# Latent attention on one core: DMA transposes in block 0, an fp16 output stage and moved pieces

## The chip, the cores and the metric

The kernel runs on one NeuronCore of one Trainium2 chip. The metric is the device time of one execution in microseconds; a kernel's time is the median of its runs.

## The reference

For 2048 tokens of 512 channels the program computes one transformer layer: latent attention (16 heads, head width 128 plus 64 rotary columns, causal), a residual and a layer norm, then a linear layer with a residual and a second layer norm.

```python
cq = rms_norm(x @ w_qa.T, q_a_ln_w)                  # 2048 x 384
q_nope, q_pe = split((cq @ w_qb.T) by head)          # 128 + 64 columns per head
ckv = x @ w_kva.T                                    # 2048 x (128 + 64)
ckv_l, k_pe = rms_norm(ckv[:, :128], kv_a_ln_w), rotate(ckv[:, 128:])
k_nope, v = split((ckv_l @ w_kvb.T) by head)         # 128 + 128 columns per head
scores = (q_full @ k_full.T) * 192 ** -0.5           # causal
attn = softmax(scores) @ v @ w_o.T                   # 2048 x 512
y = layernorm(x + attn)
out = layernorm(y + y @ (weight * scale_weight[:, None]).T + bias)
```

The inputs and the output are fp32. The kernel writes most operands as a sum of a high and a low part and adds three products (high by high, high by low, low by high).

## The kernel before

**Tiling.** The 2048 tokens are four blocks of 512 queries (`b`), the 16 heads eight pairs (`p`), each block four tiles of 128 (`qt` or `t`). A pair's scores against the keys up to the diagonal lie in PSUM, their softmax is written as fp16 high and low parts (`hl`), and SP's DMA queue turns these by `dma_start_transpose` into `PT` (block 0) or `ring` (blocks 1 to 3), from which TensorE multiplies them by the latent values `V`. So the attention leaves, for each pair, a latent output `o` of 128 x 1024 per block, which is stored in DRAM (`ot_d`) and read back in the output stage. `values` runs some units behind the softmax (`lag` is 4 in block 0, at most 3 later).

**Block 0** (0 to about 283 us) also does all projections. A written plan places pieces of them between the units of attention: "F" takes a piece of the query projections, "X" one tile of `project_x`, "W" a piece of the weight preparation. `project_x(hb)` handles 256 tokens: for each of two tiles of 128 it multiplies x into the latent keys (`kvr`), the rotary key (`kp`) and the latent queries (`pc`); the reciprocal norms `rk` are taken; `cq_finish` writes the scaled queries (`nq`, L364), `kv_finish` the scaled keys (`nk`) and, split in two, `V`. TensorE then turns `nq` (three 128 x 128 transposes a tile, `turn_cq`, L377) and `nk` and `kp` (`turn_k`, L384 and L385). ScalarE and VectorE split what was turned into `cqst` and `Kn`; `cqst` is stored to `cq_d`, for the block's queries later. The turns of a tile are run after the products of the next one (`turns`, `last_turn`).

**Blocks 1 to 3** (about 283 to 1284 us) are attention: scores (L626), the exponential (L679 on ScalarE), the split of the probabilities (L700 on ScalarE, L703 on VectorE), values (L756), and between them the next pair's query products (L584) and rotary products (L497, multiplied by the cosines and sines on VectorE, L502). In the last pair of block 3, `prepare_output` starts the output stage: it loads `wo`, the latents of block 0, and multiplies the value weights into `w_o` (`value_output`, L286, products `ps_wo`, result `wvo`). Eight steps `k` make up a pair there; `at` says at which of them a `filler` is taken. A load that is put off (`put_off`) is issued by SP ahead of the next transposes.

**Output stage** (about 1284 us to the end). For each block the eight pairs are added up in four accumulators `acc` (one for each tile `t`, L1057): 6 products of 512 columns a pair and tile, in fp32r, 24 a pair. Each pair's latents are loaded (`latent_load`) and split into `oh` (ScalarE, L74) and `ol` (VectorE, L75) by `latent_split`, one pair ahead. Then `residual` adds x (L1148), `first_norm` takes mean and variance on VectorE (L1138, L1140), their power of -1/2 on GpSimd (L292, L293), and the norm on VectorE (L1143). `ffn` turns the result (`tp`, L1159), splits it (`xt`), adds the bias on GpSimd (`xb`, L1163), multiplies by `fw` (12 products, L1169), adds, norms and stores. The ffn pieces of a block are taken between the products of the next block (`late`, `advance`); TensorE's order there is the program's own. In the last block the tiles are finished one after another, with pairs 2 to 7 split ahead (`ohl` holds those of pairs 4 to 7).

**What orders the work.** Every engine runs its own instructions in order. Where the program does not fix it (`manual_schedule`, `keep_in_program_order`), a scheduler chooses the order of each engine when the kernel is built.

Of the kernel before, what the change touches and what calls it, by code (L numbers as in the profile page):

```python
# [19 lines left out]
P = 128  # L20
# [14 lines left out]
C_TOP = 20100.0  # L35
TINY = 1.0e-30
# [18 lines left out]
def mla_block(ctx: ExitStack, tc: tile.TileContext, a, out):  # L55
# [10 lines left out]
    def split16(src, h, l, scale):  # L66

        nc.scalar.activation(h, src, AF.Copy, scale=scale)
        nc.vector.scalar_tensor_tensor(l, src, scale, h, ALU.mult, ALU.subtract)  # L69
# [11 lines left out]
    cq_d = [dram.tile([P, 2, LT, QB], F16, name=f"cq_d{b}") for b in range(NB)]  # L81
# [21 lines left out]
    kvln_o = const.tile([P, 1], F32, name="kvln_o")  # L103
    nc.vector.tensor_scalar_mul(kvln_o, kvln, 1.0 / (V_UP * P_UP))
# [14 lines left out]
    V = [kv.tile([P, 2, 4, P], F16, name=f"V{b}") for b in range(NB)]  # L119
# [3 lines left out]
    with tc.tile_pool(name="ps_w", bufs=1, space=PSUM) as ps_w:  # L123
        ramp = V[3][:, 0].rearrange("p t d -> p (t d)")
        nc.vector.memset(ramp, 0.0)
        idle = ps_w.tile([P, 512], F32, name="idle")
        for _ in range(10):
            nc.tensor.matmul(idle, ramp[:, :P], ramp, start=True, stop=True)
# [39 lines left out]
    def first_scales():  # L168

        sq = small.tile([P, 1], F32, tag="sq1", name="sq1")  # L170
        nc.vector.tensor_tensor(sq, kvln, kvln, ALU.mult)
        tot = small.tile([P, 1], F32, tag="tot", name="tot")
        column_total(tot, sq, 1)
        root(kvn, tot)
        nc.vector.tensor_scalar(kvn, kvn, C_TOP, None, ALU.mult)

# [104 lines left out]
    def value_output(p, pool, tag):  # L281

        wvo = state["wvo"][p]
        for j in range(2):
            ps = pool.tile([P, HID], F32, tag=tag, name=f"ps_wo{2 * p + j}")
            nc.tensor.matmul(ps, state["wv"][:, 2 * p + j], state["wo"][2 * p + j], start=True, stop=True)  # L286
            split(ps, wvo[:, 0, j, :], wvo[:, 1, j, :], kvln_o)
            yield

# [52 lines left out]
    def kv_finish(hb, i, kvr, rk):  # L342
# [4 lines left out]
        vh, vl = V[b][:, 0, t, :], V[b][:, 1, t, :]  # L347
# [18 lines left out]

    def inverse_rms(ms, n=2):
# [11 lines left out]

    def turn_k(hb, flip, k):  # L380
# [7 lines left out]
        if hb < 2:  # L388
            split16(kf, Kp0[:, 0, cols], Kp0[:, 1, cols], ks[0])
        split16(pt[:, 0].rearrange("p a c -> p (a c)"), Kn[:, 0, cols], Kn[:, 1, cols], K_UP)  # L390
        nc.scalar.activation(Kr[:, cols], kf, AF.Copy)
        if hb >= 2:
            nc.scalar.activation(junk[:, :256], kf, AF.Square, accum_out=ksum[:, hb + 2 : hb + 3])
# [14 lines left out]

    def project_x(hb, wkv, wqa):

        b, half_of = hb // 2, slice(hb % 2 * 256, hb % 2 * 256 + 256)
        x, csk = xsplit.pop(hb)
        flip = []
        st = pa2.tile([P, 2, LT, 256], F16, tag="st", name=f"cqst{hb}")

        def turn(i, nq):
            turn_cq(hb, i, nq, st[:, :, :, i * P : (i + 1) * P], "m")
            if i:
                nc.sync.dma_start(cq_d[b][:, :, :, half_of], st)
                turn_k(hb, flip, "m")  # L420

        for i in range(2):
            ms = small.tile([P, 2], F32, tag="ms", name="ms")
            kvr, kp = kv_products(hb, i, x, wkv, csk, "m", ms[:, 0:1])
            pc = cq_products(hb, i, x, wqa, "m", ms[:, 1:2])
            rk = inverse_rms(ms)
            nq = cq_finish(pc, rk[:, 1:2])
            flip.append((kv_finish(hb, i, kvr, rk[:, 0:1]), kp))
            last_turn()
            turns.append(lambda i=i, nq=nq: turn(i, nq))  # L430
            if i == 0:
                next_x(hb + 1)
# [33 lines left out]
    def load_block(b):  # L466
        if b == NB:
            return
        cq = prj.tile([P, 2, LT, QB], F16, tag="cq", name=f"cq{b}")
# [22 lines left out]
    def rope_products(w, cq, cs, prod, ps, x, cols):  # L492

        n = 0
        for lt in range(LT):
            for i, k in ((0, 0), (0, 1), (1, 0)):
                nc.tensor.matmul(  # L497
                    ps, w[:, i, lt, x * P : (x + 1) * P], cq[:, k, lt, cols], start=n == 0, stop=n == 3 * LT - 1
                )
                n += 1  # L500
        for k in range(2):
            nc.vector.tensor_tensor(prod[:, k, x, cols], ps, cs[:, k ^ x, cols], ALU.mult)  # L502
# [37 lines left out]
    def project_pe(b, g):  # L540
# [7 lines left out]
        for x in range(2):  # L548
            ps = psum["m"].tile([P, QB], F32, tag="m", name=f"ps_pe{b}_{g}_{x}")
            rope_products(w, cq, cs, prod, ps, x, every)  # L550
# [28 lines left out]
    def nope_products(w, cq, qn, ps, j, cols, scale):  # L579

        n = 0
        for lt in range(LT):
            for i, k in ((0, 0), (0, 1), (1, 0)):
                nc.tensor.matmul(  # L584
                    ps, w[:, i, lt, j * P : (j + 1) * P], cq[:, k, lt, cols], start=n == 0, stop=n == 3 * LT - 1
# [159 lines left out]
    def values(b, p, qt, nk, PT):  # L745
# [5 lines left out]
        for k in range(kts):  # L751
# [3 lines left out]
            for i, l in ((0, 0), (0, 1), (1, 0)):  # L755
                nc.tensor.matmul(  # L756
                    ps[:, :256], vt[:, i, k % 4, :], v[:, :, l, k, :], start=n == 0, stop=n == 3 * kts - 1
# [50 lines left out]
    with tc.manual_schedule(engines={ET.PE}):  # L808
# [17 lines left out]
        def turn_queries(hb, nqs, k):  # L826
            for i, nq in enumerate(nqs):
                o = hb * 256 + i * P
                turn_cq(hb, i, nq, state["cq"][:, :, :, o : o + P], k)
# [45 lines left out]
    def rest_of_x():  # L875
        for i in range(2, 8):
            yield from project_x(i, wkv, wqa)
        last_turn()
        yield
# [26 lines left out]
    def units(pool, ring, b):  # L906
        lag = min(ring.shape[1] // (2048 * (b + 1)) - 1, 3) if b else 4

        for p in range(NPAIR):
# [15 lines left out]
            if b == NB - 1 and p == NPAIR - 1:  # L925
# [4 lines left out]
                state["wvo"] = [pcr.tile([P, 2, 2, HID], F32R, name=f"wvo{p}", bufs=1) for p in range(EARLY)]  # L930
                for i in range(EARLY):
                    fillers.append(value_output(i, psum["m"], "m"))
                at = (3, 4, 6, 7)
            for qt in range(4):
# [25 lines left out]
                else:  # L960
                    for j in range(2):
# [8 lines left out]
                        if 2 * qt + j in at:  # L970
                            fill()
                        run_values(lag)
# [34 lines left out]
    EARLY = 2  # L1007
    ohl = []

    def latent_load(b, p, by=nc.sync.dma_start):  # L1010
        o = state["o", b, p] = state["pcr"].tile([P, 4, 256], F32, tag="o", name=f"o{b}_{p}")
        by(o, ot_d[b][p])

    def latent_split(b, p):
        if b == NB - 1 and p >= 4:
            oh, ol = ohl[p - 4]
        else:
            oh = state["pcr"].tile([P, 4, 256], F32R, tag="oh", name=f"oh{b}_{p}")
            ol = state["pcr"].tile([P, 4, 256], F32R, tag="ol", name=f"ol{b}_{p}")
        split(state.pop(("o", b, p)), oh, ol)  # L1020
        return oh, ol

    def latent(b, p):
        latent_load(b, p)
        return latent_split(b, p)
# [8 lines left out]
    def prepare_output(b, p, k):  # L1034
# [6 lines left out]
        if p == NPAIR - 1:  # L1041
            if k == 0:
                load_wo(0, blk, "qn", put_off)
            if k in (0, 1):
                latent_load(0, k, put_off)
            if k == 4:
                load_wo(1, state["pcr"], "wo")
            if k in (2, 5):
                cuts[0, k // 3] = latent_split(0, k // 3)
# [3 lines left out]
    def accumulate(acc, p, t, oh, ol):  # L1053
        for j in range(2):
            c = slice(j * P, (j + 1) * P)
            for n, (l, i) in enumerate(((oh, 0), (oh, 1), (ol, 0))):
                nc.tensor.matmul(  # L1057
                    acc,
                    l[:, t, c],
                    state["wvo"][p][:, i, j, :],  # L1060
# [22 lines left out]
    with tc.manual_schedule(engines={ET.PE, ET.SP}), ExitStack() as ctx_f:  # L1083
        for b in range(1, NB):
            with ExitStack() as ctx_s:
# [7 lines left out]
                units(pools, ring, b)  # L1093
# [5 lines left out]
        wvo += [pcq.tile([P, 2, 2, HID], F32R, name=f"wvo{EARLY + i}") for i in range(2)]  # L1099
# [21 lines left out]
    wvo += [pc.tile([P, 2, 2, HID], F32R, name=f"wvo{p}") for p in range(EARLY + 2, NPAIR - 1)]  # L1121
    wvo.append(state["pcr"].tile([P, 2, 2, HID], F32R, tag="wo", name="wvo7", bufs=1))
# [4 lines left out]
    fw = pc.tile([P, 2, KT, HID], F32R, name="fw")  # L1127
    ohl[:] = [[pc.tile([P, 4, 256], F32R, name=f"ohl{p}_{i}") for i in range(2)] for p in range(4)]

    def load_fw(kt):  # L1130
        raw = pc.tile([P, HID], F32, tag="xb", name=f"fraw{kt}", bufs=2)
        nc.scalar.dma_start(raw, a["fw"][:, kt])
        nc.vector.tensor_tensor(raw, raw, fsc, ALU.mult)
        split(raw, fw[:, 0, kt, :], fw[:, 1, kt, :])

    def layer_norm(dst, src):
        st = small.tile([P, 6], F32, tag="bn", name="bn")
        nc.vector.bn_stats(st, src)  # L1138
# [4 lines left out]
        nc.vector.tensor_scalar(dst, src, mv[:, 0:1], r, ALU.subtract, ALU.mult)  # L1143

    def residual(b, t, acc):
        x = pc.tile([P, HID], F32, tag="x", name=f"x{b}_{t}", bufs=4)
        nc.sync.dma_start(x, a["x"][4 * b + t])
        nc.vector.tensor_tensor(x, acc, x, ALU.add)  # L1148
        return x

    def first_norm(b, t, x):
        x1 = pc.tile([P, HID], F32, tag="x1", name=f"x1_{b}_{t}", bufs=4)
        layer_norm(x1, x)
        return x1

    def ffn(t, x1):
        pt = ps_f.tile([P, KT, P], F32, tag="tp", name=f"tp{t}")
        for kt in range(KT):
            nc.tensor.transpose(pt[:, kt, :], x1[:, kt * P : (kt + 1) * P], ident)  # L1159
        xt = pc.tile([P, 2, KT, P], F32R, tag="xt", name=f"xt{t}", bufs=2)  # L1160
# [115 lines left out]
```

## Time and profile before

| | us |
|---|---|
| median of 3 runs | 1543.92 |
| lowest and highest | 1543.46, 1544.02 |
| profiled execution | 1545.92 |
| its span in the profile | 1544.1 |
| TensorE busy in it | 1487.5 |
| VectorE busy | 1170.2 |
| ScalarE busy | 927.7 |
| GpSimd busy | 343.6 |

The profile is one execution. PE is TensorE's products, PEld its weight loads, which run beside them; DVE is VectorE, ACT ScalarE, POOL GpSimd, SP the engine whose queue issues most transfers. A row of the page reads: line, engine, operation, output <- inputs, shapes, how many; busy time and mean ns of one; then the idle time of that engine just before these instructions, and what ended most of it. The duration of a product includes its way through the array, so the pace of a series of products is read from the distance of their starts. Busy shares of a window are upper bounds of work done.

### The profile page before, as it was taken

To read this page: it belongs to the slowest core of one execution; us is meant where nothing else is said; L and a number is where in the kernel's file an instruction comes from. 1 tells how busy PE (TensorE), PEld (TensorE's weight loads), DVE (VectorE), ACT (ScalarE), POOL (GpSimd) and SP (SyncE) were. 2 spreads that over 40 slices of the span, in tenths; PEclk is the share of its full clock that TensorE was granted. 3 is DMA by queue.
4 is the path that set the end of the run, shared out by engine and by line. 5 is a ranking of instruction groups with operands and counts; after the bars stand their busy time and mean duration, and the time that the engine had idled before them with its cause. 6 is when DMAs were issued, how large, how long until landed. Compare 5 with 4: busy or idle time off the path is not lost. (4 is left out here: it accounts for less than half of the span.)

```text
span 1544.1 us, 24523 instructions
## 1 busy us (share of the span) xinstructions
PE 1487.5 (96%) x9100; PEld 1000.2 (65%) x9100; DVE 1170.2 (76%) x2181; ACT 927.7 (60%) x1684; POOL 343.6 (22%) x398
## 2 busy tenths in 40 slices
PE   8889898999999999999999999999999989999997
PEld 6667664566665566666665566666666647788886
DVE  4887788888888888888897877778877865555564
ACT  6677775667775777767775666666667654321120
POOL 4223221441306405050042402302200000032132
PEclk9899999999999999999999999999999999999999
DMA  5457465778897887888886787887779888433230
GB/s 199 145 135 186 126 165 116 152 150 160 167 190 149 170 156 153 164 156 164 171 172 138 150 158 154 148 161 146 156 158 184 148 192 228 129 117 118 94 116 35
DMA packets 614872, 234.56 MB, mean 152 GB/s; under 512 B 569696, under 2 KB 593248, under 8 KB 614112
## 3 DMA queue, kind: packets, MB, share of 16 engines
q1 hardware_dynamic: 613440, 231.26, 69.4%
q8 instruction: 71, 1.16, 0.3%
q10 hardware_dynamic: 1008, 1.18, 0.3%
q0 software_dynamic: 304, 0.56, 0.2%
q14 instruction: 49, 0.40, 0.1%
HBM read 62.33 MB, written 28.05 MB: 59 GB/s over the span
## 5 line engine op out<-in xcount | busy, mean ns | idle before, releaser
L626 PE MATMUL s<-Kn,qn 128*128 128x512 f16 (+5 forms) x1920 | 465.8, 349 | 20.0 <-ACT pr L679 9.0
L679 ACT ACTIVATE pr<-s,bias,er 128x1024 f32<-128x1024 f32 (+3 forms) x320 | 324.0, 1015 | 194.5 <-DVE bias L673 144.4
L703 DVE SCALAR_TENSOR_TENSOR hl<-pr,inv,hl 128x1024 f16<-128x1024 f32 (+7 forms) x320 | 357.2, 1137 | 30.5 <-ACT hl L700 26.9
L756 PEld LDWEIGHTS <-V 128*128 128x128 f16 x3264 | 318.4, 98 | 84.2 <-issue 6.9
L756 PE MATMUL o<-ring,V 128*128 128x256 f16 x3024 | 361.1, 273 | 2.1 <-DMA ring<-hl 1.8
L700 ACT ACTIVATE hl<-pr,inv 128x1024 f16<-128x1024 f32 (+7 forms) x320 | 294.2, 959 | 88.6 <-ACT pr L679 30.6
L663 DVE TENSOR_REDUCE neg<-s 128x1 f32<-128x1024 f32 (+3 forms) x320 | 316.9, 993 | 37.3 <-PE s L626 34.1
L626 PE MATMUL s<-Kp,pe 128*128 128x512 f16 (+5 forms) x1280 | 342.3, 350 | 0.0
L626 PEld LDWEIGHTS <-qn 128*128 128x128 f16 x1920 | 188.2, 98 | 166.3 <-issue 25.6
L626 PEld LDWEIGHTS <-pe 128*128 128x128 f16 x1280 | 125.3, 98 | 106.6 <-issue 0.7
L584 PE MATMUL ps_qn<-cq,wq 128*128 128x512 f16 (+1 forms) x594 | 140.9, 386 | 6.5 <-DVE inv L689 2.2
L1057 PE MATMUL acc<-wvo,oh 128*128 128x512 f32 x448 | 143.6, 402 | 0.5 <-ACT pr L679 0.5
L571 POOL TENSOR_TENSOR pe<-prod,ph 32x512 f16<-32x512 f32 x88 | 123.8, 1407 | 5.7
L562 POOL TENSOR_TENSOR prod<-prod 128x512 f32<-128x512 f32 x11 | 13.9, 1268 | 457.8 <-DVE prod L502 457.8
L584 PEld LDWEIGHTS <-wq 128*128 128x128 f16 x594 | 60.0, 101 | 70.2 <-issue 13.3
L1057 PEld LDWEIGHTS acc<-wvo,oh 128*128 128x128 f32 x448 | 83.2, 188 | 21.3 <-issue 3.3
L1057 PE MATMUL acc<-wvo,ol 128*128 128x512 f32 x224 | 88.2, 394 | 0.0
L691 DVE TENSOR_SCALAR inv<-sums 128x1 f32<-128x1 f32 x128 | 26.9, 210 | 68.7 <-ACT pr L679 68.1
L75 DVE TENSOR_TENSOR ol<-o,oh 128x1024 fp32r<-128x1024 f32 x28 | 38.9, 1388 | 45.0 <-ACT oh L74 44.9
L74 ACT ACTIVATE oh<-o 128x1024 fp32r<-128x1024 f32 x28 | 29.7, 1059 | 70.8 <-PE acc L1057 50.1
L761 ACT ACTIVATE ot<-o 128x256 f32<-128x256 f32 x128 | 48.2, 378 | 38.9 <-PE o L756 32.0
L497 PE MATMUL ps_pe<-cq,wpe 128*128 128x512 f16 (+1 forms) x306 | 69.4, 372 | 1.2 <-DVE wpe L69 0.9
(180 smaller groups left out, 1618.7 us busy)
## 6 DMA issues: line engine op xcount, KB each, us to landing
ot_d<-ot SPq DMA_DIRECT2D x128, 128.0 KB, 2.4
o<-ot_d SPq DMA_DIRECT2D x32, 512.0 KB, 3.6
wq<-wq_d SPq DMA_DIRECT2D x30, 384.0 KB, 3.5
wpe<-wpe_d SPq DMA_DIRECT2D x15, 384.0 KB, 3.8
wo<-in_wo_dram SPq DMA_DIRECT2D x4, 1024.0 KB, 5.7
x<-in_x_dram SPq DMA_DIRECT2D x16, 256.0 KB, 3.8
out_dram<-xb SPq DMA_DIRECT2D x16, 256.0 KB, 2.0
xr<-in_xT_dram SPq DMA_DIRECT2D x12, 256.0 KB, 3.5
```

The lines of the kernel that those rows point to most:

```text
L75: nc.vector.tensor_tensor(l, ps, h.bitcast(F32), ALU.subtract)
L497: nc.tensor.matmul(ps, w[:, i, lt, x * P : (x + 1) * P], cq[:, k, lt, cols], start=n == 0, stop=n == 3 * LT - 1)
L571: nc.gpsimd.tensor_tensor(pe[64 + 32 * x : 96 + 32 * x, j, :], rp[q, x, :], ph[q, 0, x, :], ALU.subtract)
L584: nc.tensor.matmul(ps, w[:, i, lt, j * P : (j + 1) * P], cq[:, k, lt, cols], start=n == 0, stop=n == 3 * LT - 1)
L626: nc.tensor.matmul(ps[:, :w], lhs, K[:, i, c0 : c0 + w], start=n == 0, stop=n == 4)
L663: nc.vector.tensor_reduce(neg[:, ti : ti + 1], v, axis=AX.XY, op=ALU.max, negate=True)
L679: nc.scalar.activation(pr[:, c0 : c0 + n * w].rearrange("p (a c) -> p a c", a=n), v, AF.Exp, bias=bias, scale=r, accum_out=sums[:, ti : ti ...
L700: nc.scalar.activation(hl[:, 0, c], pr[:, c], AF.Copy, scale=inv)
L703: nc.vector.scalar_tensor_tensor(hl[:, 1, c], pr[:, c], inv, hl[:, 0, c], ALU.mult, ALU.subtract)
L756: nc.tensor.matmul(ps[:, :256], vt[:, i, k % 4, :], v[:, :, l, k, :], start=n == 0, stop=n == 3 * kts - 1)
L761: nc.scalar.activation(ot, ps[:, :256], AF.Copy)
L1057: nc.tensor.matmul(acc, l[:, t, c], state["wvo"][p][:, i, j, :], start=p == 0 and j == 0 and n == 0, stop=p == NPAIR - 1 and j == 1 and n ...
```

## The change

In block 0, for the token tiles from 512 on, the queries and keys are scaled and split first (`ct`, `V`) and turned by `dma_start_transpose` on SP, 16 bit, high and low part in one transfer; TensorE turns only the rotary keys (`turn_kp`). `cq_d` is stored per tile of 128, and `V` and `cq` have the tile as their first axis.

The output stage runs in fp16. The norms of the value weights, of `w_o` and of `fw` are taken and divided out ahead of the splits: `output_norms` reads these weights during block 1 (ten pieces, each squared on ScalarE two steps after its load), and `back` and `fback` multiply them in again. The load of a latent stands two pairs ahead of its use, its split is held in program order, and the latents of block 3's pairs 2 to 7 are split during block 2. The last tile is done in two halves of 256 columns.

In the last pair the loads, splits and fillers are at other steps. The rotary products on VectorE are kept in program order from block 1 on.

```diff
     def project_x(hb, wkv, wqa):
...
-            rk = inverse_rms(ms)
-            nq = cq_finish(pc, rk[:, 1:2])
-            flip.append((kv_finish(hb, i, kvr, rk[:, 0:1]), kp))
+            rk = scaled_rms(ms)
+            ct = pa2.tile([P, 2, LT * P], F16, tag="ct", name=f"ct{hb}_{i}")
+            st = pa2.tile([P, 2, LT, P], F16, tag="st", name=f"st{hb}_{i}")
+            split16(pc, ct[:, 0], ct[:, 1], rk[:, 1:2])
+            nc.sync.dma_start_transpose(
+                st.rearrange("p a l q -> p (a l) q"), ct.rearrange("p a c -> p (a c)")
+            )
+            while stores:
+                stores.pop(0)()
+            stores.append(lambda t=t, st=st: tc.keep_in_program_order(nc.sync.dma_start(cq_d[b][:, t], st)))
+            split16(kvr, V[b][:, t, 0], V[b][:, t, 1], rk[:, 0:1])
+            o = hb * 256 + i * P
+            nc.sync.dma_start_transpose(Kn[:, :, o : o + P], V[b][:, t].rearrange("p a d -> p (a d)"))
             last_turn()
-            turns.append(lambda i=i, nq=nq: turn(i, nq))
-            if i == 0:
+            if i:
+                turns.append(lambda: turn_kp(hb, kps, "m"))
+            else:
                 next_x(hb + 1)
...
+    def output_norms(pool):
+        pieces = [a["wv"][:, 8 * i : 8 * i + 8] for i in range(2)] + [a["wo"][:, 2 * i : 2 * i + 2] for i in range(8)]
...
+                w = pool.tile([P, 1024], F32, tag="nw", name=f"nw{n}")
+                put_off(w.rearrange("p (a c) -> p a c", a=8 if n < 2 else 2), pieces[n])
...
+                tc.keep_in_program_order(
+                    nc.scalar.activation(w, w, AF.Square, accum_out=sums[:, n - 2 : n - 1])
+                )
...
         for k in range(2):
-            nc.vector.tensor_tensor(prod[:, k, x, cols], ps, cs[:, k ^ x, cols], ALU.mult)
+            pin(nc.vector.tensor_tensor(prod[:, k, x, cols], ps, cs[:, k ^ x, cols], ALU.mult))
...
-                at = (3, 4, 6, 7)
+                at = (2, 4, 5, 6)
...
+                        if b == 1 and p >= 2 and j == 1:
+                            next(norms, None)
...
     def latent_split(b, p):
-        if b == NB - 1 and p >= 4:
-            oh, ol = ohl[p - 4]
+        if b == NB - 1 and p >= CUT:
+            oh, ol = ohl[p - CUT]
         else:
-            oh = state["pcr"].tile([P, 4, 256], F32R, tag="oh", name=f"oh{b}_{p}")
-            ol = state["pcr"].tile([P, 4, 256], F32R, tag="ol", name=f"ol{b}_{p}")
-        split(state.pop(("o", b, p)), oh, ol)
+            oh = state["pcr"].tile([P, 4, 256], F16, tag="oh", name=f"oh{b}_{p}")
+            ol = state["pcr"].tile([P, 4, 256], F16, tag="ol", name=f"ol{b}_{p}")
+        split16(state.pop(("o", b, p)), oh, ol, kvo, tc.keep_in_program_order)
...
-            if k in (0, 1):
-                latent_load(0, k, put_off)
+            if k in (1, 2):
+                latent_load(0, k - 1, put_off)
             if k == 4:
                 load_wo(1, state["pcr"], "wo")
-            if k in (2, 5):
-                cuts[0, k // 3] = latent_split(0, k // 3)
+            if k in (3, 7):
+                cuts[0, k // 7] = latent_split(0, k // 7)
...
             for p in range(0 if b else EARLY, CUT if last else NPAIR):
-                nxt = order[NPAIR * b + p + 1]
+                i = NPAIR * b + p
+                for nxt in order[i + 1 : i + 3]:
+                    if nxt < (NB - 1, CUT) and nxt not in cuts and ("o", *nxt) not in state:
+                        latent_load(*nxt)
+                nxt = order[i + 1]
                 if nxt not in cuts:
-                    cuts[nxt] = latent(*nxt)
-                for t in range(4):
+                    cuts[nxt] = latent_split(*nxt)
+                if b == NB - 2 and p >= CUT:
+                    cuts[NB - 1, p] = latent_split(NB - 1, p)
+                if b == NB - 2 and CUT - 1 <= p < NPAIR - 1:
+                    latent_load(NB - 1, p + 1)
+                for t in range(3 if last else 4):
                     accumulate(accs[t], p, t, *cuts[b, p])
...
                 if b == 0 and p >= 4:
-                    load_fw(p - 4)
+                    next(fw_steps)
...
+            ends = [accs[3], ps_a.tile([P, HID], F32, tag="acc", name="acc3_4")]
+            for i, c in enumerate(parts(2)):
+                for p in range(NPAIR):
+                    accumulate(ends[i], p, 3, *cuts[b, p], c)
+                    if (i, p) in ((0, 6), (1, 2)):
+                        advance()
```

`load_fw` is now four steps, one a pair from pair 4 of block 0 on: the loads; the products with the scale and their squares; the norm; the four splits.

## The prediction

> **What bounds the kernel now.** I read the page first, then windows of 40 us, then the timeline at the places that the change touches. The page (the span; busy us, share and instructions by engine; two groups as busy us, mean ns of one | idle before):
>
> ```profile
> span 1544.1 us, 24523 instructions
> PE 1487.5 (96%) x9100; PEld 1000.2 (65%) x9100; DVE 1170.2 (76%) x2181; ACT 927.7 (60%) x1684; POOL 343.6 (22%) x398
> L1057 PEld LDWEIGHTS acc<-wvo,oh 128*128 128x128 f32 x448 | 83.2, 188 | 21.3 <-issue 3.3
> L626 PEld LDWEIGHTS <-qn 128*128 128x128 f16 x1920 | 188.2, 98 | 166.3 <-issue 25.6
> ```
>
> TensorE is the bound: work taken from it, or a wait of it, counts; work elsewhere counts only if TensorE ends up waiting. Where it is not full, the windows say (length, busy us and instructions by engine, granted clock, DMA share, GB/s):
>
> ```profile
> core 0: us, PE busy (x) PEld busy (x) DVE busy (x) ACT busy (x) POOL busy (x), PEclk, DMA share, GB/s
> 80.00:120.00 40.00, 35.22 (x235) 25.20 (x233) 34.76 (x90) 32.15 (x91) 11.99 (x19) 0.94 0.61 159
> 240.00:280.00 40.00, 33.99 (x184) 18.39 (x183) 31.74 (x74) 21.07 (x45) 5.06 (x4) 0.91 0.50 108
> 1240.00:1280.00 40.00, 34.00 (x199) 20.24 (x197) 29.15 (x40) 25.33 (x37) 0.00 (x0) 0.96 0.82 172
> ```
>
> Block 0 (to 283 us) leaves some 33 us of TensorE idle, in gaps of 0.9 to 4.9 us. From there the idle is 16.4 us, of which one gap has 5.05, in the last pair of heads:
>
> ```profile
> 1248.66 1.12 PE L626 MATMUL s<-Kn,qn 128*128 128x384 f16 x3 [5.05 <-ACT pr L679]
> 1249.58 0.84 PE L626 MATMUL s<-Kp,pe 128*128 128x384 f16 x2
> 1250.22 1.17 PE L626 MATMUL s<-Kn,qn 128*128 128x384 f16 x3
> ```
>
> The output stage (1284 to the end) has almost no gap. So there the length of a matmul counts, and whatever the change lets TensorE wait for.
>
> **Output stage in fp16.** One block is 192 products into `acc`, 48 of the ffn and 16 transposes. The first transposes of two blocks start at 1361.02 and 1417.99: 56.97 us, less 16 x 0.109 = 1.74, over 240 gives 0.230 us a product, start to start. The fp16 products of the same 512 columns with a weight load each (L626) stand 0.216 apart. 768 + 192 products x 0.014 = **-13.4 us**. The weight load falls from 188 to 98 ns, beside the products. The halves of the last tile (256 columns, 0.1095 in L756) double the count and leave the sum.
>
> **What the new order makes late.** `latent_split` is pinned to program order. In the built instruction stream of VectorE the split of the next block's pair 1 now stands behind the four residuals and all four first norms (from block 0 to 1 also behind four `fw` splits, from 2 to 3 behind one `ohl` split). Before, it stood ahead of the norms. The boundary from block 1 to 2, VectorE, then GpSimd:
>
> ```profile
> 1408.66 0.69 DVE L1148 TENSOR_TENSOR x<-acc,x 128x512 f32<-128x512 f32 x1
> 1409.27 1.28 DVE L1138 BATCH_NORM_STATS2 bn<-x 128x6 f32<-128x512 f32 x2
> 1410.46 1.21 DVE L75 TENSOR_TENSOR ol<-o,oh 128x1024 fp32r<-128x1024 f32 x1
> 1411.58 0.55 DVE L1143 TENSOR_SCALAR x<-x,mv,lnr 128x512 f32<-128x512 f32 x1
> ...
> 1416.96 1.17 DVE L1143 TENSOR_SCALAR x<-x,mv,lnr 128x512 f32<-128x512 f32 x2 [0.63 <-POOL lnr L293]
> ```
>
> ```profile
> 1412.21 1.59 POOL L1163 TENSOR_TENSOR xb<-x,fb 128x512 f32<-128x512 f32 x1 [2.20 <-DVE x L1143]
> 1413.77 0.21 POOL L292 TENSOR_SCALAR rs_t<-mv 128x1 f32<-128x1 f32 x1
> 1413.95 1.29 POOL L1163 TENSOR_TENSOR xb<-x,fb 128x512 f32<-128x512 f32 x1
> 1415.21 1.18 POOL L292 TENSOR_SCALAR rs_t<-mv 128x1 f32<-128x1 f32 x1
> 1416.36 1.18 POOL L293 TENSOR_TENSOR lnr<-rs_t,nhalf 128x1 f32<-128x1 f32 x2
> ```
>
> Norms 2 and 3 wait for GpSimd, which does two `xb` additions before their `lnr`; its order stays so. Before, that wait held nobody. Let E be the end of a block's last product (42 products before the transposes at 1417.99: E = 1408.45). Norm 0 can start at E + 2.0 (behind the statistics), norm 2 at 0.63 + 3.0 (xb, rs_t, xb) + 0.2 + 0.56 = 4.4 later (the 1.18 of `rs_t` ran beside an `ol` split that now comes after, so I take 0.2), norm 3 ends at E + 7.4, `ol_1` takes 1.2: E + 8.6. TensorE needs it after 24 + 2 products, E + 5.6: **+3.0**. For the others I count VectorE's queue from the end of `ol_0`, E - 2.95 (a step of 24 x 0.216 = 5.2 less `oh` 1.06 and `ol` 1.2), with residuals and `fw` splits 0.65 apart, statistics 0.6. From 0 to 1: 4 residuals, 4 `fw` splits, 3 statistics and 2 small ones, 7.2: norm 0 at E + 4.3, `ol_1` 6.6 later as above, E + 10.9: **+5.3**. From 2 to 3: 4 residuals, one `ohl` split of 1.15, 4 statistics and 3 small ones, 6.45: norm 0 at E + 3.5, `ol_1` at E + 10.1, and a step has only 18 products, so it is needed at E + 4.3: **+5.8**. Sum **+14.1**; were GpSimd no limit, the VectorE rows alone would give 2.5 + 0 + 2.3 = 4.8, which is the low end; 15 is the high one.
>
> After its 5.05 us gap TensorE did ten 384-column products in 3.16 us (1248.66 to 1251.82), against 10 x 0.163 (three quarters of 0.216): 1.5 us lost to a lower clock. Two of the three new gaps are as long: **+3.1** (0 to 4.6).
>
> The Trainium skill (TensorE: Matmul & The Clock Gate, Part 1) says that the clock drops to half only after an idle window of about 3.4 us. By it the 3.0 us gap and the tail's wait cost nothing, while block 0 here shows a granted clock of 0.91 over 40 us with no gap over 2.4; going by that row they would cost up to 1.5 each, and my range holds both.
>
> **Block 0 turned by DMA.** Removed: 36 `ps_qt` and 12 `ps_kt` transposes at 0.109 spacing, 5.2 us of TensorE; on VectorE 12 `nq` (0.616) and 6 `Kn` splits (0.41), 9.9 us; on ScalarE 12 `nk` (0.398) and 6 `Kn` (0.383), 7.1 us. The groups of the two transposes also carry 1.9 and 3.2 us of idle before them. Added on SP: 24 transposes, 12 stores for 6. Transposes of block 0 hold SP for 1.2 to 2.4 us there (one 4.1): 29 to 58 us more, on a queue about a third busy; results are needed first in block 1. All of the TensorE time and a little of its waits: **-6** (0 to -10).
>
> **Last pair.** In the 5.05 gap ScalarE stood 7.11 us for `o<-ot_d`, issued at 1235.65 right behind a 1 MB `wo` load. Now `wo` goes at step 0, `o` at steps 1 and 2, the splits at 3 and 7. The gap and its cold 1.5 us are 6.6; part of the wait is the ring transposes on SP (7.39 us for one there), which stay: **-4** (0 to -6.6).
>
> **Small ones.** Norms in block 1: ten loads of 512 KB on SP (3.6 us in the row of that size), ten squares (nearest row L679, 1.0) on ScalarE, with 28 of 40 us busy, four small POOL steps: **+0.5** (0 to 2). `fw`: its scale load landed 7.3 us late for VectorE already; the multiplications come one pair later, TensorE a little sooner: **+0.5** (0 to 1.5). Pinned rotary products: their places in VectorE's stream move by a few instructions, TensorE's neighbours stay: **0** (-1 to 1). Tail: halved x, statistics, norm and `xt` save about 1.9 us of the chain after the last product, but ffn 14 (2.7 us), which filled the wait for the last norm, now runs before the last `acc` ends: **+0.8** (-1 to 3.4). Layouts of V and cq: nothing.
>
> **Sum.** -13.4 + 14.1 + 3.1 - 6 - 4 + 0.5 + 0.5 + 0.8 = -4.4. The profiled run took 1545.92 (span 1544.1), 2.0 over the median of 1543.92; the forecast is 1541.5 for it, **1539.5** as median. 0.2%, or 3.1 us, is about what a measurement tells from no change.
>
> **Rivals.** (1) GpSimd is no limit at the boundaries: 4.8 for 14.1 and no cold clock, 1539.5 - 9.3 - 3.1 = 1527.1. For it: POOL spans are rough. Against: VectorE's own idle of 0.63 names it. (2) Slower: block 0 waits for SP. Each of 12 transposes waits in order for its `ct` (ScalarE, then VectorE), and the transposes of probabilities behind it come late. If each tile holds TensorE for 1.2 us, its shortest issue, block 0 gives -5.2 + 14.4 = +9.2 for -6: 1554.7. It makes the kernel slower from 0.56 us a tile. Against: values run four units behind. (3) Nothing is won in block 0 and the last pair, since ScalarE and VectorE set both: 1549.5. (4) fp16 products keep 0.230: 1552.9. L626 speaks against it.
>
> **Chances.** Forecast 0.46, (1) 0.22, (3) 0.15, (2) 0.13, (4) 0.04. Of the forecast's own range (1533 to 1546) three quarters (0.35) are faster and most of the rest same; with (1) that makes 0.57 faster. A third of (3), nearer the forecast, counts as same; the rest of (3), (2) and (4) slower. Faster 0.57, same 0.16, slower 0.27. From (1) to (3): 1527 to 1549.5.
>
> **What would show it.** Products of L1057's successor 0.216 apart; three TensorE gaps ahead of pair 1 of blocks 1 to 3 of about 5, 3 and 6 us, released by `ol`; no gap of 5 us near 1245; 5 us less TensorE work in block 0. No such gaps, or block 0 not shorter, makes the forecast wrong.

## The result, and the profile after

The changed kernel takes 1563.21 us (median of 4, 1562.35 to 1566.95), the kernel before 1543.97 on the same chip: ratio 1.0127, interval 1.0109 to 1.0146. It is 19 us slower; I had forecast 4 us faster. The profiled execution took 1562.73, its span is 1560.9.

The page after, in the same columns:

```profile
span 1560.9 us, 24629 instructions
PE 1476.8 (95%) x9116; PEld 918.5 (59%) x9116; DVE 1171.9 (75%) x2181; ACT 938.2 (60%) x1695; POOL 348.2 (22%) x404
L1124 PEld LDWEIGHTS <-oh 128*128 128x128 f16 x424 | 42.4, 100 | 52.9 <-issue 11.3
L562 PE MATMUL ps_pe<-cq,wpe 128*128 128x512 f16 (+1 forms) x306 | 73.5, 388 | 11.3 <-DVE prod L567 9.5
L1124 PE MATMUL acc<-wvo,ol 128*128 128x512 f16 (+1 forms) x212 | 81.8, 386 | 15.6 <-DVE ol L72 15.6
```

The two groups of products in the page before:

```profile
L497 PE MATMUL ps_pe<-cq,wpe 128*128 128x512 f16 (+1 forms) x306 | 69.4, 372 | 1.2 <-DVE wpe L69 0.9
L1057 PE MATMUL acc<-wvo,ol 128*128 128x512 f32 x224 | 88.2, 394 | 0.0
```

TensorE is busy 10.7 us less than before, and the span is 16.8 longer: its idle time grew by 27.5. The fp16 weight loads take 100 ns for 188. Two rows name most of this growth. Products into `acc` waited 15.6 us for `ol` splits (0.0 before), and rotary products 9.5 us for `prod` (1.2 us of idle for all reasons before).

The three gaps at the boundaries of the output stage, and the pace behind the middle one (timeline of TensorE):

```profile
1369.22 0.61 PE L1124 MATMUL acc<-wvo,ol 128*128 128x512 f16 x1 [6.41 <-DVE ol L72]
1427.85 0.61 PE L1124 MATMUL acc<-wvo,ol 128*128 128x512 f16 x1 [3.31 <-DVE ol L72]
1428.25 1.06 PE L1124 MATMUL acc<-wvo,oh 128*128 128x512 f16 x2
...
1432.61 0.60 PE L1258 MATMUL tp<-ident,x 128*128 128x128 f32 x4
1487.45 0.61 PE L1124 MATMUL acc<-wvo,ol 128*128 128x512 f16 x1 [5.87 <-DVE ol L72]
```

They are 6.4, 3.3 and 5.9 us, where I had worked out 5.3, 3.0 and 5.8. From 1427.85 to 1432.61 stand 16 products, 3.46 us at 0.216, done in 4.76: even the gap of 3.3 us cost 1.3 us of clock (the granted clock is 0.50 from 1427.8 to 1430.0 us).

I cut both executions at the same unit of work, the first score reductions of a block or pair on VectorE and the first product into `acc`. The lengths in us:

| stretch | before | after | difference | forecast |
|---|---|---|---|---|
| block 0 | 263.2 | 250.2 | -13.0 | -6 |
| block 1, pairs 0 and 1 | 53.8 | 52.2 | -1.6 | 0 |
| block 1, pairs 2 to 7 | 173.8 | 187.5 | +13.7 | +0.5 |
| block 2 | 337.8 | 347.6 | +9.8 | 0 |
| block 3, pairs 0 to 6 | 396.9 | 399.2 | +2.3 | 0 |
| last pair | 59.1 | 55.1 | -4.0 | -4 |
| output stage | 259.6 | 269.1 | +9.5 | +5.1 |

Block 0 won more than forecast. It was lost between 302 and 838 us, where I had put half a microsecond. Two waits there, and what stood ahead of `prod` in the second (timelines of TensorE, VectorE and ScalarE, block 1):

```profile
343.25 2.10 PE L649 MATMUL ps_qn<-cq,wq 128*128 128x512 f16 x9 [1.75 <-ACT ot L826]
...
362.81 1.46 PE L562 MATMUL ps_pe<-cq,wpe 128*128 128x512 f16 x6
...
366.17 0.43 PE L691 MATMUL s<-Kp,pe 128*128 128x320 f16 x2
369.36 1.01 PE L562 MATMUL ps_pe<-cq,wpe 128*128 128x512 f16 x2 [2.75 <-DVE prod L567]
```

```profile
365.23 1.28 DVE L768 SCALAR_TENSOR_TENSOR hl<-pr,inv,hl 128x1024 f16<-128x1024 f32 x1 [0.69 <-ACT hl L765]
366.64 0.30 DVE L697 TENSOR_TENSOR s<-s,maskb 128x128 f32<-128x128 f32 x1
366.98 0.82 DVE L728 TENSOR_REDUCE neg<-s 128x1 f32<-128x640 f32 x1
...
368.04 1.27 DVE L567 TENSOR_TENSOR prod<-ps_pe,cs 128x512 f32<-128x512 f32 x2
```

```profile
364.05 1.14 ACT L765 ACTIVATE hl<-pr,inv 128x1024 f16<-128x1024 f32 x1
365.10 1.04 ACT L312 ACTIVATE nw<-nw 128x1024 f32<-128x1024 f32 x1
366.04 0.19 ACT L312 ACTIVATION_READ_ACCUMULATOR nw<-nw 128x1 f32 x1
366.13 0.87 ACT L744 ACTIVATE pr<-s,bias,er 128x640 f32<-128x640 f32 x1
```

Here ScalarE has no idle time between the softmax steps, and a square with its read takes 1.03 us (365.10 to 366.13) of that chain. The `prod` of the pair stands in VectorE's order behind a split that waited 0.69 us for ScalarE, and behind the mask and the reduction of scores that TensorE finished at 366.60, after `ps_pe`. So it starts at 368.04, though the products that it reads had ended by 364.3. The other wait, at 343.25, is for the copy `ot`, which stood on ScalarE behind a square that waited 0.88 us for its load.

### The profile page after: what moved, and what is told of

Read it like the earlier page. It is cut to its first block, busy times and chain, and to the rows that moved or that the text cites. A ratio compares the mean times of both kernels' runs of the same rounds, so it can differ in the third digit from the quotient of the medians.

```text
span 1560.9 us, 24629 instructions
## 1 busy us (share of the span) xinstructions
PE 1476.8 (95%) x9116; PEld 918.5 (59%) x9116; DVE 1171.9 (75%) x2181; ACT 938.2 (60%) x1695; POOL 348.2 (22%) x404
## 5 line engine op out<-in xcount | busy, mean ns | idle before, releaser
L649 PE MATMUL ps_qn<-cq,wq 128*128 128x512 f16 (+1 forms) x594 | 137.6, 379 | 4.4 <-ACT ot L826 2.2
L1124 PE MATMUL acc<-wvo,oh 128*128 128x512 f16 (+1 forms) x424 | 127.6, 384 | 2.6 <-ACT pr L744 2.6
L1124 PE MATMUL acc<-wvo,ol 128*128 128x512 f16 (+1 forms) x212 | 81.8, 386 | 15.6 <-DVE ol L72 15.6
L562 PE MATMUL ps_pe<-cq,wpe 128*128 128x512 f16 (+1 forms) x306 | 73.5, 388 | 11.3 <-DVE prod L567 9.5
L71 ACT ACTIVATE xt<-tp 128x512 f16<-128x512 f32 (+1 forms) x17 | 9.7, 573 | 121.8 <-PE tp L1258 107.8
L1124 PEld LDWEIGHTS <-oh 128*128 128x128 f16 x424 | 42.4, 100 | 52.9 <-issue 11.3
L631 POOL CAST pe<-prod 32x512 f16<-32x512 f32 x88 | 65.0, 738 | 11.7 <-PE o L821 8.4
```

The source lines that it names most:

```text
L562: nc.tensor.matmul(ps, w[:, i, lt, x * P : (x + 1) * P], cq[:, tiles(cols), k, lt], start=n == 0, stop=n == 3 * LT - 1)
L631: nc.gpsimd.tensor_copy(pe[32 * x : 32 * x + 32, j, :], rp[q, x, :])
L649: nc.tensor.matmul(ps, w[:, i, lt, j * P : (j + 1) * P], cq[:, tiles(cols), k, lt], start=n == 0, stop=n == 3 * LT - 1)
L1124: nc.tensor.matmul(acc[:, cols], l[:, t, c], state["wvo"][p][:, i, j, cols], start=p == 0 and j == 0 and n == 0, stop=p == NPAIR - 1 and j ...
```

## The experiments

The times in this section come from several chips; each ratio is against the kernel before on the same chip, and a difference in us is that of the ratios times 1545.

**The pinned latent splits.** An instruction is called pinned here when the program keeps it in its own order on its engine, and free when the scheduler places it. Theory: the three pins or additions (latent splits, rotary products, norms) each cost TensorE time. Rival: blocks 1 and 2 give back what block 0 won, whatever the pins. In the first kernel only the splits ahead for block 3 stay pinned:

```diff
-        split16(state.pop(("o", b, p)), oh, ol, kvo, tc.keep_in_program_order)
+        pin = tc.keep_in_program_order if b == NB - 1 and p >= CUT else lambda ins: ins
+        split16(state.pop(("o", b, p)), oh, ol, kvo, pin)
```

> The changed kernel (1563.2 us) with the latent splits of a block's own pairs left to the scheduler; only the splits ahead for block 3 stay pinned. The split of pair 1 of the next block then stands ahead of the first norms again. Theory A (the pinned splits cause the three gaps of 6.4, 3.3 and 5.9 us at the block boundaries, 15.6 us, and some 4 us of lower clock behind them): all three gaps go, 1544 us (1542 to 1548). Rival B (the boundary waits on GpSimd's norm chain or on DMA of the latents, whatever the order): gaps stay, within 3 us of 1563.

Measured: 1543.51, ratio 0.9981 (0.9972 to 0.9991), 22.6 us less than the changed kernel. The output stage fell from 269.1 to 249.0 us, and no gap is left at the boundaries between its blocks. VectorE from block 0 to 1:

```profile
1358.94 1.27 DVE L72 SCALAR_TENSOR_TENSOR ol<-o,kvo,oh 128x1024 f16<-128x1024 f32 x1
1360.13 1.00 DVE L1239 TENSOR_SCALAR x<-x,mv,lnr 128x512 f32<-128x512 f32 x2
...
1365.38 1.16 DVE L1239 TENSOR_SCALAR x<-x,mv,lnr 128x512 f32<-128x512 f32 x2 [1.95 <-POOL lnr L334]
```

The split stands ahead of the norms, and the wait for GpSimd (1.95 us) is still there but holds nobody. So it was the place of the split, as the prediction had it.

**The pinned rotary products.** `rope_products` gets no pin in any block:

```diff
-            rope_products(w, cq, cs, prod, ps, x, every, tc.keep_in_program_order if b else lambda ins: ins)
+            rope_products(w, cq, cs, prod, ps, x, every, lambda ins: ins)
```

> The changed kernel with the rotary products left to the scheduler in all blocks. Theory A (pinned products hold TensorE's two buffers, 9.5 us of its waits name them, and the clock falls after them): blocks 1 and 2 shorter by 8 to 12 us, 1553 us. Rival B (blocks 1 and 2 give back what block 0 won since another limit, VectorE or ScalarE, sets their pace and block 0 only starts them earlier): the waits take other names, 1561 to 1565.

Measured: 1557.45, ratio 1.0077 (1.0056 to 1.0098), 7.7 us less. Pairs 2 to 7 of block 1 take 180.3 for 187.5 and block 2 339.7 for 347.6, so these lost 15 us. But block 3 took 3.9 us more, by a longer gap at its start (6.0 us for 3.3) that the last experiments bear on, and so the time lies between the two forecasts.

**The norms.** This leaves out part of the computation, the loads and the sums of squares:

```diff
+        nc.vector.memset(sums[:, 0:2], 8.0)
+        nc.vector.memset(sums[:, 2:10], 0.5)
         for n in range(len(pieces) + 2):
-            if n < len(pieces):
...
-                    nc.scalar.activation(w, w, AF.Square, accum_out=sums[:, n - 2 : n - 1])
...
```

> The changed kernel without the ten loads and ten squares in block 1; the sums are set to constants near the true ones, the small steps after them stay. Theory A (each square of 1.05 us and its read of the sum, 0.19, stands in ScalarE's softmax chain, with its load ahead of a transpose on SP): pairs 2 to 7 of block 1 get shorter by 6 to 12 us, 1555 us (1551 to 1558). Rival B (block 1 loses its lead to a limit that was there before): within 3 us of 1563.

Measured: 1558.35, ratio 1.0083 (1.0066 to 1.0100), 6.8 us less; pairs 2 to 7 of block 1 take 181.3.

**All three.**

> The changed kernel with all three: rotary products free, no loads and squares (sums as constants), own latent splits free. Theory A, the three add up: 1563 - 19 - 10 - 8 = 1526 us (1522 to 1533), faster than the kernel before. Rival B (only the boundaries count, blocks 1 and 2 give block 0's gain back anyway): 1541 to 1546.

Measured: 1522.26, ratio 0.9849 (0.9835 to 0.9864), 23 us faster than the kernel before, though it leaves out the loads and squares of the norms, as do all versions called "all three fixes" below. The gains of the single ones sum to 37 us, the joint gain is 43. Pairs 2 to 7 of block 1 take 175.7 and block 2 338.1, within 2 us of the kernel before, and the lead of block 0 is kept: the rival falls.

**What of the norms costs.** From here on the base has two fixes, rotary products and own splits free, with the norms as in the changed kernel. The second kernel squares a fixed tile and has no loads; the third has the loads, only copies a column of each, and sets the sums to constants:

```diff
...
-                    nc.scalar.activation(w, w, AF.Square, accum_out=sums[:, n - 2 : n - 1])
+                    nc.scalar.activation(
+                        w, fixed, AF.Square, scale=1.0 if n < 4 else 0.25, accum_out=sums[:, n - 2 : n - 1]
+                    )
```

```diff
...
-                    nc.scalar.activation(w, w, AF.Square, accum_out=sums[:, n - 2 : n - 1])
+                    nc.scalar.activation(seen[:, n - 2 : n - 1], w[:, :1], AF.Copy)
```

> Rotary products free and own latent splits free, loads and squares of the norms as in the changed kernel. Theory A: dearer than all three fixes (1522.3) by what the norms cost, 6 to 8 us, so 1528 to 1531. Rival (the norms cost only in company of the pinned products, since the sum of the single gains was smaller than the joint one): within 2 us of 1522.

> As the one with two fixes, but the ten squares read a tile that stays in SBUF, filled once: no loads in block 1 for the norms (sums of about the right size). Theory S (the squares, 1.24 us each with the read of the sum, stand in ScalarE's softmax chain): the time of the two fixes, within 2 us. Rival L (the loads on SP ahead of the transposes, and ScalarE's wait for them): that of all three, 1522, within 2 us.

> As the one with two fixes, but with the ten loads only: instead of a square ScalarE copies one column of the loaded tile (some 0.2 us), sums as constants. Theory S: 1522 to 1525, what all three fixes give. Rival L: the time of the two fixes, within 2 us.

Measured: two fixes 1535.21, ratio 0.9937 (0.9921 to 0.9954); with squares alone 1527.67, 0.9883 (0.9868 to 0.9897); with loads alone 1524.81, 0.9865 (0.9851 to 0.9880). Against all three fixes that is +13.6, +5.3 and +2.5: neither theory had it, and each part costs something. In pairs 2 to 7 of block 1, where the loads and squares stand, it is 180.0, 177.6 and 179.2 against 175.7: +4.3, +1.9 and +3.5, so there the two together cost no more than their sum. What goes beyond it stands in blocks 2 and 3, where only the version with two fixes has long gaps at the starts (see below; 340.1 and 402.8 us, against 337.5 and 397.3 in both others).

**Other places for the norms.** The squares without `keep_in_program_order`; the norms in block 3; the loads issued by GpSimd:

```diff
-                        if b == 1 and p >= 2 and j == 1:
+                        if b == 3 and p >= 1 and j == 1:
...
```

```diff
-                put_off(w.rearrange("p (a c) -> p a c", a=8 if n < 2 else 2), pieces[n])
+                nc.gpsimd.dma_start(w.rearrange("p (a c) -> p a c", a=8 if n < 2 else 2), pieces[n])
```

> Two fixes, squares in block 1 left to the scheduler. Theory A (the place of a square in ScalarE's order decides, as for the other two pins): 1526 to 1531. Rival (the squares and loads cost the same wherever in block 1 they stand): 1533 to 1537.

> Two fixes, with the loads and squares of the norms in pairs 1 to 6 of block 3 in place of pairs 2 to 7 of block 1. Theory A (a square costs what ScalarE's softmax chain is short of; in block 3 TensorE works 4 to 5 us per softmax unit and ScalarE has 13 of 40 us free, in block 1 some 12): 1524 to 1528 us, of which 2.5 for the loads. Rival (in any block a pinned square delays the exponentials by its length): 1533 to 1537, as in block 1.

> Two fixes with the norms in block 1, the ten loads issued by GpSimd's queue in place of SP's, without being put off. If SP's queue (a load ahead of a transpose of probabilities) makes the loads dear: 1527 to 1530, the squares' 5.4 alone. If the squares wait for data or memory traffic counts wherever it is issued: 1533 to 1537, as with SP.

Measured: unpinned 1533.02 (0.9923, 0.9908 to 0.9938), in block 3 1539.84 (0.9965, 0.9952 to 0.9978), by GpSimd's queue 1525.23 (0.9873, 0.9856 to 0.9891). ScalarE's free time in a block is no measure: block 3 was the dearest place (pairs 0 to 6 take 412.0 us for 402.8, against 5.0 won in block 1). Nor is the pin the price: the free squares make pairs 2 to 7 of block 1 longer, 186.5 us for 180.0, and the kernel is no slower only because its gaps at the starts of blocks 2 and 3 are short. The version by GpSimd's queue is 9.9 us faster than the two fixes, but only 2.0 of it stand in block 1 (178.0 for 180.0, about what squares alone take); 9.0 stand in blocks 2 and 3, again by short gaps at their starts. So SP's queue costs some 2 us in block 1; that it makes the long gaps is not shown, since the version with loads alone has its loads on SP and short gaps. The version by GpSimd's queue computes all that the changed kernel does and is 20 us faster than the kernel before. The answer on its tile `nw` gives its loads of `wo` (line, engine, operation and count; durations min/median/max in ns; first and last start) and who waited for the tile (us, times):

```profile
L307 POOL DMA_DIRECT2D nw<-in_wo_dram x8: 527/528/650, 197.9 to 374.0; - x8
  POOL nw L307: 31.3, 5
```

The loads are issued from 197.9 us on, as early as a buffer is free, and not ahead of the transposes on SP. GpSimd stood 31.3 us for buffers that the squares had not left; TensorE had no wait that names it.

**The last pair and the tail.** With all three fixes, the last pair's old steps; then the last tile in one piece (the inverse of those parts of the change):

```diff
-                at = (2, 4, 5, 6)
+                at = (3, 4, 6, 7)
...
-            if k in (3, 7):
-                cuts[0, k // 7] = latent_split(0, k // 7)
+            if k in (2, 5):
+                cuts[0, k // 3] = latent_split(0, k // 3)
```

```diff
...
-            late.append(ffn(4 * b + 3, first_norm(b, 3, residual(b, 3, halves, 2), 2), 2))
+            late.append(ffn(4 * b + 3, first_norm(b, 3, residual(b, 3, accs[3]))))
```

> All three fixes (1522.3 us) with the last pair's loads, splits and fillers at their old steps. By the prediction's step (4 us won there) and the last pair's length in the profiles (59.1 us before, 55.1 to 55.7 in every version with the new steps): 1526 us (1525 to 1528). Rival (the pair is only shorter because its work moved behind it, into the wait of 2.6 to 2.8 us ahead of the first accumulation): within 1.5 us of 1522.

> All three fixes (1522.3 us) with the last tile in one piece of 512 columns: whole residual, statistics, norm, transposes, ffn and store. The last ffn before it still stands ahead of the end of the last accumulation. The chain after the last product then takes about 1.9 us more by the rows of the kernel before (each halved step waited for one half only): 1524 us. Rival (the halves double the small steps and win nothing): within 1 us of 1522.

Measured: old steps 1523.58 (0.9861, 0.9846 to 0.9876), whole tile 1525.55 (0.9871, 0.9855 to 0.9888): +1.9, within the intervals of each other, and +3.4, where the intervals just overlap. TensorE with the old steps, then with the new ones:

```profile
1236.99 1.12 PE L684 MATMUL s<-Kn,qn 128*128 128x384 f16 x3 [5.68 <-ACT pr L737]
```

```profile
1273.56 0.59 PE L1118 MATMUL acc<-wvo,oh 128*128 128x512 f16 x2 [2.83 <-ACT pr L737]
```

The old steps bring the 5.7 us gap back and the pair takes 59.3 for 55.6 us; but the new steps leave a 2.8 us gap at the first accumulations, and the output stage takes 251.0 for 247.6. The gain is nearly given back. The tail, TensorE, whole and in halves:

```profile
1511.15 1.09 PE L1252 MATMUL tp<-ident,x 128*128 128x128 f32 x4 [3.73 <-DVE x L1232]
1512.93 5.01 PE L1261 MATMUL ff<-fw,xt 128*128 128x512 f16 x12 [0.69 <-ACT xt L71]
```

```profile
1508.91 0.73 PE L1252 MATMUL tp<-ident,x 128*128 128x128 f32 x4 [2.77 <-DVE x L1232]
1509.79 4.44 PE L1261 MATMUL ff<-fw,xt 128*128 128x256 f16 x24 [0.15 <-ACT xt L71]
```

Both run the last ffn at a low clock (12 products of 512 take 2.75 us elsewhere). The halves make the wait a microsecond shorter and shorten the one before the ffn from 0.69 to 0.15 us.

**The rotary pin by itself.** All three fixes, with the pin on `rope_products` put back.

> Own latent splits free and no loads and squares (sums as constants), but the rotary products of blocks 1 to 3 pinned as in the changed kernel. Theory A (the pin has a price of its own, 9.5 us of TensorE waits and the lower clock after them, about 12 us): 1534 us (1530 to 1538). Rival (most of it comes only with the squares in block 1): 1524 to 1528.

Measured: 1535.57, ratio 0.9935 (0.9919 to 0.9951), 13.3 us more than with all three fixes: the pin has its own price, and the squares aren't needed for it.

**Block 0 by itself.** First the three fixes with TensorE's turns, then the kernel before with `project_x` and what it needs from the change, and nothing else of it.

> All three fixes, but block 0 as in the kernel before: TensorE turns queries and keys, 48 transposes, with fp32 scaling ahead of them (stores of cq per tile of 128). Theory A (block 0's gain of 11 to 13 us holds to the end once blocks 1 and 2 give nothing back): 1534 us (1531 to 1537). Rival (an earlier end of block 0 is lost again in block 1, whatever the pins): within 3 us of 1522.

> The kernel before with block 0's part of the change alone: queries and keys of the tiles from 512 on turned by DMA, per-tile layouts of cq and V; output stage, last pair and rotary products as before. If block 0's gain is its own (11 to 13 us by the length of block 0 in the profiles) and holds: 1544.9 - 12 = 1533 us (1531 to 1535). By my prediction's step: 1539. If the 21 us between all three fixes and the same with TensorE's turns are all block 0's: 1524.

Measured: 1543.26 (0.9987, 0.9977 to 0.9996) and 1543.95 (0.9994, 0.9983 to 1.0005). So by one comparison the DMA turns are worth 21 us, by the other nothing that can be told, while block 0's own length differs by 8.7 us in the one pair and 10.5 in the other. The kernel with block 0's part alone, TensorE and ScalarE at the start of block 3, and SP before it:

```profile
832.42 0.96 PE L650 MATMUL s<-Kn,qn 128*128 128x320 f16 x3 [6.01 <-ACT pr L703]
```

```profile
831.07 1.20 ACT L703 ACTIVATE pr<-s,bias,er 128x1024 f32<-128x1024 f32 x1 [6.40 <-DMA ring<-hl]
```

```profile
820.19 8.94 SPq L731 DMA_TRANSPOSE ring<-hl  x2
```

The first exponential of block 3 waits for the second of two transposes of block 2; from the start of the first issue to the end of the second it is 8.94 us. The same gap (6.0 to 6.1 us, and one of 2.3 to 2.4 at the start of block 2, where a split `hl` waits 1.9 to 2.0 us for a transpose) is in the kernels with the rotary products free, with two fixes, with TensorE's turns and with norms in block 3. In the changed kernel the gap at the start of block 3 is 3.3 us, also behind the second transpose. In the kernel before, with all three fixes, with free squares and with the loads by GpSimd it is 0.8 us: there the exponential waits for the first of the two. By the program the pools of a block lie where those of the last one lay, so I took its first `pr` to cover an `hl` that a transpose still reads, the last one or the one before. What decides between these two was not found: the two fixes with pinned and with free squares open the same pools, and the one waits for the second, the other for the first. The last two experiments put `pr` ahead of `hl`:

```diff
-                    ctx_s.enter_context(tc.tile_pool(name=f"{k}{b}", bufs=2, reuse_waits="tile")) for k in ("hl", "pr")
+                    ctx_s.enter_context(tc.tile_pool(name=f"{k}{b}", bufs=2, reuse_waits="tile")) for k in ("pr", "hl")
...
```

> The kernel with block 0's part alone, and the buffers of the exponentials (pr) placed ahead of those of the split probabilities (hl) in SBUF for blocks 1 to 3, so that a new block's first exponentials do not lie where the last block's transposes still read. Theory P (block 0's gain of 10.5 is lost in waits of the first exponentials of blocks 2 and 3 for transposes of the block before, 2.4 and 6.0 us of TensorE gaps): both gaps go, 1536 us (1534 to 1538). Rival (the gain is lost to SP's transposes however memory lies): 1542 to 1546.

> Two fixes, norms' loads by GpSimd's queue, and the same placement. That kernel shows only short gaps at the block starts (1.7 and 0.8 us); theory P: 1523 to 1525, 0 to 2 us faster than without. Rival (the other placement costs elsewhere, at hl): 1526 to 1530.

Measured: block 0's part alone now 1535.74, ratio 0.9932 (0.9916 to 0.9949), 9.6 us less than without, with no gap over 1 us at the start of block 3:

```profile
825.05 1.20 ACT L703 ACTIVATE pr<-s,bias,er 128x1024 f32<-128x1024 f32 x1 [0.83 <-DVE hl L727]
```

Block 3 took 6.8 us less (395.1 for 401.9). Block 2 kept its length (340.1 for 339.9): its gap shrank from 2.4 to 0.9 us, but one of 2.1 stands 11 us behind it, for 0.45 there without. So the theory held in block 3 alone. Against the kernel before, blocks 2 and 3 are within 2.5 us and block 0 is 11.0 shorter: its part is worth about 10 us, and one wait of this kind can hide it or double it in a comparison. (The kernel before with this placement was not run.) Added to the version with GpSimd's loads, whose gaps were short anyway, the placement gave 1529.56 (0.9894, 0.9870 to 0.9917; 1524.68 to 1533.56): no gain, and inside the rival's range. But blocks 2 and 3 kept their lengths there (337.5 and 396.1 us); the profiles differ in block 0 and the output stage, which the placement does not touch.

## Why the prediction was wrong, point by point

- **Output stage in fp16: right.** Products stand 0.216 us apart, and without the boundary gaps and the wait at its start the stage took 247.6 for 259.6 us (-12.0 for -13.4 and the tail).
- **Boundaries: right in kind, place and size.** The gaps are 15.6 us for 14.1; with the clock behind them 20.1 us came back when the pin went, for 17.2. The cold clock also followed the 3.3 us gap. So the Trainium skill's window of about 3.4 us (TensorE: Matmul & The Clock Gate, Part 1) is no safe bound: the row from block 0 that I set against it was the better guide. From 285 us on the traces of all the kernels together have 72 gaps of TensorE from 2.0 to 3.8 us: after 54 of them the granted clock fell to 0.5 within 4 us, after a gap of 2.27 us too (rotary products free, at 497.50), and after 18 it stayed at 1.00, once after 3.59 (rotary pin by itself, at 489.80). It fell after all 15 gaps of 5 us and more. So whether a short gap costs clock was partly luck, and a difference of a microsecond or so between two kernels can be that (1.3 us behind the 3.3 us gap).
- **Pinned rotary products: the step that failed most.** I set 0 (-1 to 1), because their places in VectorE's list moved by a few instructions. The price is 7.7 us when this pin alone goes, and 13.3 when it is put back to all three fixes. In a list kept in order the place counts by what stands ahead and waits: the reduction ahead of `prod` waited for scores that TensorE did after `ps_pe`, and the program gives `ps_pe` two buffers. I had not asked, as I did for the latent splits, when each neighbour can start.
- **Norms in block 1: the next.** 0.5 (0 to 2) for a price of 6.8 in the changed kernel and 13.6 with the other two fixed; in pairs 2 to 7 of block 1 itself it is 6.2 and 4.3, and most of the rest of the 13.6 is the wait named below as nowhere in the sum. I argued from ScalarE's 28 of 40 us. Its chain of exponentials and splits has no slack where the squares stand (no idle time from 364.05 to 367.00), and the loads stand on SP ahead of transposes; loads alone and squares alone each made block 1 longer.
- **Block 0: -6 forecast, -13 in its length, about -10 by itself.** Kernels with the same block 0 show it 10 to 13 us shorter, so the -13 is the high end. SP did carry the transposes; the slower rival by SP there did not come. TensorE's idle time in block 0 stayed at 29.8 us. Beside the 5.2 us of transposes, the granted clock rose from 0.94 to 0.96 over the first 280 us, some 5 us; what else shortened it was not taken apart.
- **A wait that was nowhere in the sum.** The starts of blocks 2 and 3 cost up to 8.4 us of gaps (2.4 and 6.0). At block 3 it goes by which transpose of the block before the first exponential waits for; in the changed kernel that gap is 3.3 us. Why a kernel waits for the one or the other stays open, and so does the gap at block 2.
- **Last pair: -4 forecast and -4.0 in the pair, but about -2 in the kernel,** since the wait moved to the first accumulation. **Tail:** +0.8 forecast for the halves; they save about 3. The +0.5 for `fw` was not taken apart.

The sum failed in blocks 1 and 2: 23.5 us stand there, where I had put 0.5.

## What to carry to other kernels

An instruction that is pinned to an engine's order costs what the instructions ahead of it wait for, not its distance in the list: write down the start of each neighbour before putting it at nothing. But leaving an instruction to the scheduler is no cure by itself: the free squares made block 1 longer. An engine's share of free time said nothing here of the chain through it; and an early stage's gain should be followed to the next place where buffers change hands, since one wait for a transfer can take it back.

## What the runs showed of the hardware

- After a gap of 3.31 us TensorE's next products stood up to twice as far apart as usual (granted clock 0.50), and 16 of them took 1.3 us more; after 3.73 us twelve products of 512 columns took 5.01 us for 2.75. Of 72 gaps of 2.0 to 3.8 us, 54 were followed by that clock and 18 were not; all 15 of 5 us and more were.
- Ten loads of 512 KB on SP and ten squares on ScalarE made pairs 2 to 7 of block 1 3.5 and 1.9 us longer alone and 4.3 together; with the loads issued by GpSimd it was 2.3.
- The two transposes at the end of block 2 take SP 8.9 us from the start of the first issue to the end of the second (block 0's part alone, all three fixes). With the first exponential of block 3 waiting for the second of them, ScalarE stood idle for 6.4 us before it; waiting for the first, for 1.2.
